# First element by seven products, its first pair's weights on their own, and three moves in the slots' order

## The chip, the cores and the metric

The kernel runs on one core of one Trainium2 chip. The metric is device time in microseconds (us) of one execution. Before the change the median of three runs is 3424.11 us (3422.17 to 3424.67). The profile comes from one further execution.

## The reference, cut to what matters

Everything is float32: 32 elements of 512 nodes with 512 features, each with its own 512 x 512 adjacency. Layer 0 is an attention with 8 heads of 64, whose weights are multiplied by the adjacency; layer 1 is a graph attention.

```python
q = x @ Wq.T + bq;  k = x @ Wk.T + bk;  v = x @ Wv.T + bv          # heads of 64
attn = softmax(q @ k.T / 8 + log(clip(adj, 1e-8)))                 # per head
x = layer_norm(x + (attn @ v) @ Wo.T + bo)
p = x @ fc_w.T + fc_b
l = (p @ q_w + q_b) + (p @ k_w + k_b).T + (1 - adj) * -1e9
out = softmax(leaky(l)) @ p + x
```

## The kernel before, in words

**Slots.** For each element b the four pairs of heads p go through slot(b, p), so there are 4 x 32 slots, the very last of which is last_slot. In one slot TensorE does the scores of pair p (score, L821, four tiles "sc"), the attention times v of the pair before it (values, L859, "po"), and the projections q and k of the next pair. Layer 1 of the element before is woven between. The order on each engine is the order in which the code calls the helpers: the schedule is manual and every engine takes its instructions in that order. Almost every helper puts work on several engines, so moving one call moves its part on TensorE (PE), VectorE (DVE), ScalarE (ACT) and the queue of SP, through which all DMAs go.

**Exponentials and factors.** ScalarE takes exp of each score tile into a tile "at" (L826). VectorE multiplies it by the clipped adjacency, held transposed in the tile cT (factors, L834); cT is loaded in blocks (load_a, L514) and turned in place (turn_a, L566). VectorE also adds the at tiles over keys ("as", L844 and L847).

**Products by four and by seven.** A product of two 2 x 2 block matrices can be done by four 128x512-wide accumulations or, with sums and differences of blocks, by seven half as wide (instead of eight). For elements 1 to 31 seven_qk (L613, into the banks a, b, c, d of two "f" tiles) and seven_v (L206, "pv_a", "pv_b", "pv_c") do this. They need three differences of blocks of x, the tile T, which differences (L594 to L597) makes, together with a change of xT in place; and three combinations of the weights, qk_s and v_s, which combine_units (L181 to L184) makes, with a change of wk and wv in place. After the products VectorE adds banks into qT, kT (L645 to L647) and v (L682, L686, L687). combine_right (L196 to L199) makes the same combinations for fc, "fc_s".

Element 0 is done otherwise: qk_units and v_units (L311, "pq", "pk", "pv") with plain products of x and whole weights. The weights' combinations stand in slot 0 of element 0 (the last one, on wk, in slot 3).

**Loads.** SP issues x of element 0 (four pieces), two biases, wq in four pieces, wk, wv (1 MB each), then the 16 block loads of the adjacency, and then wo, fc and the small rows (load_first_constants, load_a, load_constants).

**Layer 1 around the change.** layer1_rows is the rest of slot 2: it normalises the element before (L367 on ScalarE), forms its dots with uk and uq (L377, with a junk output), stores k's row to DRAM (store_k), loads it back to all partitions (load_k, into a tile "w"), and transposes the next x (L544). For b = 1 it also ends with combine_right of fc. In slot 3, softmax gives three units: logits of rows 0 and 1, of rows 2 and 3 (ScalarE L420 then VectorE L421), and weights (L427 to L432).

**The last slot.** It has layer 1 of elements 30 and 31. soft[1] of element 30 stands behind values and a first product of out. The dots of element 31 write their junk into the tile w, which is in the one buffer of tag "x" that the transposed weights eT of element 30 hold before it, read by its products z ("pz", L311). "pt_e" are transposes of the softmax weights (L304), "pg" the last products (L311), "pw" the products with wo.

Two lines show where the first element differs:

```python
next_qk = qk(0, p + 1)                   # b == 0 and p < 3
next_qk = seven_qk(b, p + 1)             # else, p < 3
```

## Time and profile before

| what | value |
|---|---|
| median of three runs | 3424.11 us (3422.17 to 3424.67) |
| profiled execution, its own time | 3423.87 us |
| its span, first to last instruction | 3422.1 us |
| TensorE busy | 3399.8 us, 99% |
| VectorE busy | 2991.7 us, 87% |
| ScalarE busy | 1392.2 us, 41% |
| DMA | 73 GB/s mean |
| mean granted TensorE clock | 0.998 |

A line of the timeline has the start in us, the duration in us, the engine, the line of the kernel, the operation, out<-in by the program's names, shapes and count, and in brackets the idle time before it with what ended it. A line of the waits has the engine and line that waited, what it waited for, the us in total, the number of times and the longest. A row of the windows has a stretch of time, then each engine's busy us and its instructions, the granted clock (1.00 is full speed), the DMA share and GB/s. A TensorE product in float32 shows two records for each call, so a product of four calls is "x8".

### The profile page before, as it was taken

The numbers are of one execution on the slowest core, as the hardware profiler recorded it, in microseconds if no ns is written. First come the engines' busy times: TensorE is split into PE (matmuls) and PEld (weight loads), VectorE is DVE, ScalarE is ACT, GpSimd is POOL, SyncE is SP. The second block draws the span as 40 slices with busy tenths as digits, with TensorE's granted clock in tenths as the row PEclk, the third lists the DMA queues.
The fourth block names the chain that finished last, engine by engine and source line by source line (L and its number), as shares of the span: only waits on it lengthen the run. The fifth ranks groups of instructions, "written<-read, shape, count | busy, mean of one in ns | idle before, by whom it ended". The sixth has DMA issues, their size and how long they took to land.

```text
span 3422.1 us, 42719 instructions
## 1 busy us (share of the span) xinstructions
PE 3399.8 (99%) x15250; PEld 2331.8 (68%) x15250; DVE 2991.7 (87%) x5239; ACT 1392.2 (41%) x2368; POOL 0.9 (0%) x9
## 2 busy tenths in 40 slices
PE   9999999999999999999999999999999999999998
PEld 3667776776677667766776677677767776776654
DVE  5889989889898898888898988989889989889885
ACT  3444443434433444434444343443344443434432
POOL 0000000000000000000000000000000000000000
PEclk9999999999999999999999999999999999999999
DMA  4244233342423433333424234343344343342420
GB/s 117 38 78 90 60 81 69 63 90 64 86 66 57 90 81 68 79 64 69 90 60 87 67 58 90 71 79 72 53 87 87 62 82 67 63 90 63 86 75 32
DMA packets 880034, 250.93 MB, mean 73 GB/s; under 512 B 806732, under 2 KB 806988, under 8 KB 879816
## 3 DMA queue, kind: packets, MB, share of 16 engines
q1 hardware_dynamic: 879816, 248.15, 35.8%
q8 instruction: 122, 2.00, 0.2%
q14 instruction: 96, 0.79, 0.1%
HBM read 181.93 MB, written 34.65 MB: 63 GB/s over the span
## 4 chain that ended last, share of the span: by engine, by line
PE 97%; DVE 1%; ACT 0%; DMA 0%; issue 0%; SPq 0%; DVEq 0%
PE f L613 22%; PE sc L821 14%; PE po L859 13%; PE pw_a L206 7%; PE pw_z_a L986 6%; PE pv_a L206 5%; PE pw_o_a L206 4%; PE pw_c L206 3%; PE pv_c L206 3%; PE pv_b L206 3%; PE pw_z_c L986 3%; PE pw_o_c L206 3%; PE pw_o_b L206 3%; PE ps L876 2%; PE pw_b L206 2%; PE pw_z_b L986 2%
## 5 line engine op out<-in xcount | busy, mean ns | idle before, releaser
L826 ACT ACTIVATE at<-sc 128x1024 f32<-128x1024 f32 x512 | 496.6, 1022 | 597.5 <-PE sc L821 596.2
L834 DVE SCALAR_TENSOR_TENSOR at<-cT,at 128x1024 f32<-128x1024 f32 x512 | 600.2, 1214 | 18.0 <-ACT at L826 17.6
L821 PE MATMUL sc<-qT,kT 64*128 64x512 f32 x2048 | 508.8, 615 | 1.4 <-DVE kT L647 1.4
L859 PE MATMUL po<-at,v 128*64 128x512 f32 x2048 | 468.1, 599 | 0.4 <-DVE at L834 0.3
L821 PEld LDWEIGHTS sc<-qT,kT 64*128 64x128 f32 x2048 | 177.7, 186 | 269.1 <-issue 269.1
L859 PEld LDWEIGHTS po<-at,v 128*64 128x64 f32 x2048 | 135.4, 136 | 317.4 <-issue 311.8
L847 DVE TENSOR_TENSOR as<-as,at 128x1024 f32<-128x1024 f32 x254 | 310.2, 1221 | 5.4
L613 PE MATMUL f<-xT,wq 128*128 128x256 f32 x992 | 261.7, 386 | 0.0
L613 PE MATMUL f<-T,qk_s 128*128 128x256 f32 x992 | 244.5, 379 | 0.0
L613 PEld LDWEIGHTS f<-xT,wq 128*128 128x128 f32 x992 | 183.9, 190 | 74.7 <-ACT at L826 52.0
L986 PE MATMUL pw_z_a<-eP,n 128*128 128x256 f32 x960 | 226.9, 379 | 1.1 <-DVE n L1023 1.1
L613 PEld LDWEIGHTS f<-T,qk_s 128*128 128x128 f32 x992 | 188.3, 190 | 25.9
L986 PEld LDWEIGHTS pw_z_a<-eP,n 128*128 128x128 f32 x960 | 180.2, 190 | 28.3 <-ACT L L998 1.5
L867 ACT COPY oT<-po 128x512 f32<-128x512 f32 x128 | 75.2, 587 | 290.0 <-PE po L859 290.0
L844 DVE TENSOR_TENSOR as<-at,at 128x1024 f32<-128x1024 f32 x128 | 154.9, 1210 | 1.1
L636 ACT ACTIVATE qT<-f,bq 128x256 f32<-128x256 f32 x124 | 58.3, 470 | 220.1 <-PE f L613 220.1
L642 ACT ACTIVATE kT<-f,bk 128x256 f32<-128x256 f32 x124 | 58.5, 472 | 195.8 <-PE f L613 195.8
L752 DVE TENSOR_TENSOR n<-pw_a,n 128x512 f32<-128x512 f32 x96 | 66.4, 691 | 77.0 <-PE pw_a L206 77.0
L613 PE MATMUL f<-T,wk 128*128 128x256 f32 x496 | 127.3, 379 | 0.0
L613 PE MATMUL f<-xT,qk_s 128*128 128x256 f32 x496 | 127.3, 379 | 0.0
L613 PE MATMUL f<-xT,wk 128*128 128x256 f32 x496 | 127.3, 379 | 0.0
L206 PE MATMUL pv_a<-wv,xT 128*128 128x256 f32 x496 | 120.4, 386 | 0.0
(255 smaller groups left out, 5804.5 us busy)
## 6 DMA issues: line engine op xcount, KB each, us to landing
cT<-in_adj_dram SPq DMA_DIRECT2D x512, 64.0 KB
R<-d SPq DMA_DIRECT2D x126, 256.0 KB
x<-in_x_dram SPq DMA_DIRECT2D x124, 256.0 KB
n<-in_x_dram SPq DMA_DIRECT2D x31, 1024.0 KB
L<-in_adj_dram SPq DMA_DIRECT2D x60, 512.0 KB
eP<-L SPq DMA_DIRECT2D x480, 64.0 KB
out_dram<-yb SPq DMA_DIRECT2D x58, 512.0 KB
w<-dk SPq DMA_DIRECT2D x32, 256.0 KB
```

Source lines behind the costliest of these rows:

```text
L206: nc.tensor.matmul(to[:, n, :], data(i, c)[:, ts(n, P)], weights[i][:, c, :], start=(first and n == 0 and c == 0), stop=(n == KH - 1 and c ...
L613: nc.tensor.matmul(to, left[i][:, c, ts(p, P)], s["B"][i][:, c, :], start=(first and c == 0), stop=(c == KH - 1), skip_group_check=True,)
L752: nc.vector.tensor_add(to, ps[name], to)
L821: nc.tensor.matmul(sc[:, j, :], s["kT", p][rows, ts(kc, P)], s["qT", p][rows, :], start=True, stop=True,)
L826: nc.scalar.activation(at, sc, AF.Exp, scale=SCALE)
L834: nc.vector.scalar_tensor_tensor(at, cT[:, kc, :].unsqueeze(1).to_broadcast([P, 2, N]), ADJ_MIN, at, ALU.max, ALU.mult,)
L844: nc.vector.tensor_add(s["as", p], s["at", p, 0], s["at", p, 1])
L847: nc.vector.tensor_add(s["as", p], s["as", p], s["at", p, kc])
L859: nc.tensor.matmul(s["po", p][j * DK : (j + 1) * DK, :], s["v"][h // 4][:, kc, ts(h % 4, DK)], s["at", p, kc][:, j, :], start=(kc == 0), s ...
L867: nc.scalar.copy(s["oT"][p], s["po", p])
L876: nc.tensor.matmul(ps[h * BL : (h + 1) * BL, :], ones[:, :BL], s["as", p + h // 2][:, h % 2, :], start=True, stop=True,)
L986: nc.tensor.matmul(ps[name][:, m, :].rearrange("p (c n) -> p c n", c=KH), left[i][:, t, ts(m, P)], right[i][:, :, ts(t, P)], start=(first ...
```

## The change

It has five parts:

- **Loads.** The first 128 columns of wq and wk, all that pair 0 of element 0 needs, are loaded on their own into "first_pair", a tile from the ring of six "at" buffers. After them wv, wq and wk come whole, in this order, each as one DMA.
- **Element 0.** Pair 0's q and k are plain products with these columns. differences(0) and all combinations of wv, wq and wk follow at once, ahead of turn_a. v is then done by seven products (two units in slot 0 between the scores, two after them), and q and k of pairs 1 to 3 by seven_qk.
- **combine_right of fc** (slot 2 of element 1) stands ahead of the additions of next_qk, no longer at the end of layer1_rows.
- **soft[1] of element 30** in the last slot stands between the two halves of values.
- **The dots of element 31** write their junk into the tile R of that element; the tile w is taken only for load_k.

```diff
-    def load_first_constants():
+    def load_first_constants(pair):
         K["bq"] = load_col(const, bq, "bq")
         K["bk"] = load_col(const, bk, "bk")
-        K["wq"] = load_weight(wqT, "wq", 4)
+        for dst, w in zip(pair, (wqT, wkT)):
+            nc.sync.dma_start(out=dst, in_=w[:, :P].rearrange("(c p) d -> p c d", p=P))
+        K["wv"] = load_weight(wvT, "wv")
+        K["wq"] = load_weight(wqT, "wq")
         K["wk"] = load_weight(wkT, "wk")
-        K["wv"] = load_weight(wvT, "wv")
...
-            run(values(b, p - 1) if p > 0 else values(last, 3) if last >= 0 else first_v[1:2])
+            run(values(b, p - 1) if p > 0 else values(last, 3) if last >= 0 else first_v[:2])
...
-                if b == 0:
-                    run(combine_qk()[1:])
...
-            if b == 0 and p < 3:
-                next_qk = qk(0, p + 1)
-            elif p < 3:
+            if p < 3:
                 next_qk = seven_qk(b, p + 1)
...
                 if b == 0:
-                    run(combine(K["wv"], K["v_s"])[:1] + combine_qk()[:1])
-                run(next_qk)
-                if b == 0:
-                    run(first_v[2:] + combine(K["wv"], K["v_s"])[1:])
+                    run(first_v[2:] + next_qk)
                 else:
+                    run(next_qk)
...
             if b == 1:
+                combine_right(K["fc"], K["fc_s"])
                 run(next_qk[2:])
...
-            if b == 1:
-                combine_right(K["fc"], K["fc_s"])
...
             vs[0]()
+            soft[1]()
             vs[1]()
             rest[0]()
-            run(soft[1:])
+            run(soft[2:])
...
-            ks, qs = dots(b)
+            ks, qs = dots_units(S[b], small, S[b]["R", 0][:, 1, :], b)
             run(ks)
-            k_rows(b)
+            store_k(S[b], small, dram, b)
+            load_k(S[b], work(b)[:, 1, :])
...
-        load_first_constants()
+        pair = act.tile([P, 2, N], FP, tag="at", name="first_pair", bufs=6)
+        pair = [pair[:, i, :].rearrange("p (c d) -> p c d", c=DC) for i in range(2)]
+        load_first_constants(pair)
...
-        first_v = v(0)
-        run(qk(0, 0) + first_v[:1])
+        run(first_qk(*pair))
+        differences(0)
+        run(combine(K["wv"], K["v_s"]) + combine_qk())
+        first_v = seven_v(0)
         turn_a(range(NC))
```

More of the change, by code (lines that the diff above doesn't have):

```diff
@@ L320, in v_units, with qk_units @@
         return [lambda c=c: unit(c) for c in range(NC)]
-    def qk_units(s, wk, p, qT, kT, psum, name):
+    def qk_units(s, wq, wk, p, qT, kT, psum, name):
         def unit(w, b, to, what):
@@ L328, in qk_units @@
         return [
-            lambda: unit(K["wq"], K["bq"], qT, "q"),
+            lambda: unit(wq, K["bq"], qT, "q"),
             lambda: unit(wk, K["bk"], kT, "k"),
@@ L575, in qk_tiles, with first_qk @@
                 S[b][w, p] = act.tile([P, N], FP, tag=w, name=f"{w}_{b}_{p}", bufs=2)
-        def v(b):
-            v_tiles(b)
-            return v_units(S[b], K["wv"], ps_m, b)
-        def qk(b, p):
-            qk_tiles(b, p)
-            s = S[b]
-            return qk_units(s, K["wk"], p, s["qT", p], s["kT", p], ps_m, b)
+        def first_qk(wq, wk):
+            qk_tiles(0, 0)
+            s = S[0]
+            return qk_units(s, wq, wk, 0, s["qT", 0], s["kT", 0], ps_m, 0)
         def differences(b):
@@ L1082, in work @@
             return S[b]["w"]
-        def dots(b):
-            w = work(b)
-            return dots_units(S[b], small, w[:, 0, :], b)
-        def k_rows(b):
-            store_k(S[b], small, dram, b)
-            load_k(S[b], S[b]["w"][:, 1, :])
         def softmax(b):
@@ L1443, in general @@
             kT = act.tile([P, N], FP, tag="kT", name=f"g_kT_{p}")
-            for u in qk_units(s, s["wk"], p, qT, kT, ps_m, "g"):
+            for u in qk_units(s, K["wq"], s["wk"], p, qT, kT, ps_m, "g"):
                 u()
```

## The prediction

> **What bounds the kernel now.** I read the page's busy shares first, then the list of what TensorE waited for over the whole span, then the timeline of each wait with the engine that ended it, and last the granted clock around them.

> ```profile
> PE 3399.8 (99%) x15250; PEld 2331.8 (68%) x15250; DVE 2991.7 (87%) x5239; ACT 1392.2 (41%) x2368; POOL 0.9 (0%) x9
> ```
> ```profile
> PE pt_x L560 <- DMA n<-in_x_dram: 3.7, 1, 3.7
> PE pv_c L206 <- DVE T L594: 2.6, 1, 2.6
> PE pt_e L304 <- ACT cT L432: 2.5, 4, 1.4
> PE pk L311 <- DMA wk<-in_wkT_dram: 2.3, 1, 2.3
> PE sc L821 <- DVE kT L647: 1.4, 1, 1.4
> ...
> PE pw_c L206 <- DVE oT L928: 1.1, 1, 1.1
> ```

> TensorE is busy 99%, and each of these waits happens once (the third in four pieces): at the start, in slot 2 to 3 of element 1, and in the last slot. Between them the kernel is TensorE's work end to end, 52.5 us an element, and the diff changes no instruction of elements 2 to 30. So I price four places: the loads, element 0, element 1, the tail.

> ```profile
> 13.63 5.37 PE L311 MATMUL pk<-xT,wk 128*128 128x512 f32 x8 [2.34 <-DMA wk<-in_wkT_dram]
> 18.83 3.60 PE L311 MATMUL pv<-wv,xT 128*128 128x512 f32 x8
> ```
> ```profile
> 174.30:176.80 2.50, 0.00 (x1) 0.00 (x0) 2.47 (x4) 1.55 (x3) 0.00 (x0) 1.00 0.90 344
> 176.80:178.00 1.20, 1.13 (x4) 0.99 (x5) 1.13 (x3) 0.27 (x1) 0.00 (x0) 0.85 0.06 21
> 178.00:179.00 1.00, 1.00 (x4) 0.79 (x3) 1.00 (x3) 0.00 (x0) 0.00 (x0) 0.50 0.00 0
> ```
> In the second fence, the third figure from the right is the granted clock (0.50 in the last row). **An idle TensorE costs twice**: after the waits of 2.34 and 2.57 us it runs at half clock for about 4 us. pk takes 5.20 us to the next start, 18.83 - 13.63, where the same eight records later take 3.44: 1.76 lost. pv_c and the two f products after it take 4.38 (176.87 to 181.25) against 2.58: 1.80 lost. After the 1.35 us wait before sc at 164.89 the clock stays 1.00, so the step lies between 1.4 and 2.3 us of idleness.

> [...]

> **The change, part by part.**

> *Loads.* All go through SP's one queue. The two pair tiles (256 KB each, runs of 512 B) stand where the first two 256 KB pieces of wq stood. pq never waited for those: its second quarter started at 8.44. Price of the pair's 0.52 MB: runs of 2 KB move 314 to 385 GB/s in the first 15 us, the 128 B runs of cT some 115; so 1.5 us to 4.6. Per run that is 94 and 17.8 ns on each of 16 engines; a straight line between gives 33 ns for 512 B, 248 GB/s, 2.1 us, which I take. pq then starts 0.2 late (0 to 1.3), and pk finds its weights. All of wv, wq, wk and adjacency land 2.1 later: the transposes of cT (L566), now at 18.19, 20.09, 22.14 and 24.50, can go up to 26.6.

> [...]

> *Element 0, slot 0.* Before: pk's issue ends at 18.83. After: 7.58 + 0.2 + 2 x 3.44 = 14.66, **-4.17** (wait, lost clock, and 0.27 of drain that the wait was counted from). From there to the scores of pair 1 it was 43.76 - 18.83 = 24.93. Now: kT is no longer covered by pv, so sc waits for ScalarE, 0.2 + 0.69 + 0.15 = 1.04; four score tiles 3.82; seven v products at 1.725 (pv_b to pv_a, 93.29 to 95.02) 12.08 in place of four at 3.44; seven f products at 0.865, 6.05 in place of two at 3.44; changes of tile 0.2; and the additions into kT before sc, 1.1 (in slot 2 of element 1 the same handover takes 1.52 from the last f record's slot to sc, with ScalarE busy on other rows). Sum 24.29, **-0.64**.

> VectorE must keep up. It does three differences under pq, the fourth after pk (14.9), combine of wv 4 x 0.72 to 18.4, of wq and wk 4 x 1.24 from about 18.7 to 23.7 (wk lands about 18.6), the transposes to 27.3, four factors at 1.17, one sum 1.22, three v additions 1.95: 35.2. TensorE's last f product ends at 37.6. Slack 2.0 us: up to 2.0 more of load delay is free.

> *Slots 1 to 3.* Slot 1: f 6.05 for 6.87, -0.82; f now waits for the second exponential to free its bank, +0.45; the additions end under ps_bvwo (3.44), so sc does not wait. **-0.37.** Slot 2: **-0.82**, the additions under ps_bfc. VectorE runs about 1.0 us later against TensorE in slot 2, so T's first difference comes 0.15 late for pv_c in slot 3: **+0.15**; the one operation on wk leaves that slot (-1.22 on VectorE), and its 3.38 us of idleness before L682 absorbs the rest. If it did not, up to 1 us more.

> Element 0 together: -4.17 - 0.64 - 0.37 - 0.82 + 0.15 = **-5.85** (bounds -3 and -7).

> *Element 1, slot 2.*

> ```profile
> 163.66 0.42 DVE L645 TENSOR_TENSOR qT<-f,qT 128x256 f32<-128x256 f32 x1 [3.62 <-ACT kT L642]
> ...
> 173.48 0.69 DVE L196 TENSOR_TENSOR fc_s<-fc 128x512 f32<-128x512 f32 x1
> ...
> 175.53 0.68 DVE L199 TENSOR_TENSOR fc<-fc 128x512 f32<-128x512 f32 x1
> 176.14 0.68 DVE L594 TENSOR_TENSOR T<-xT 128x512 f32<-128x512 f32 x1
> ```
> The four operations of combine_right stand ahead of the difference that pv_c waits for. Moved before the additions of next_qk they take 2.7 us inside the 3.62 that VectorE stands idle for ScalarE's kT; behind them wait only L645 to L647. If they overran, sc would wait up to 2.7 longer. T starts at 173.48 and pv_c at 174.25 instead of 176.87: 2.62, and the clock's 1.80: **-4.4** (bounds -2.6 without the clock, -4.5). Late next: the copy into pv_b behind the w activations on ScalarE, at 177.1, needed at 177.7.

> *Tail.*

> ```profile
> 3331.96 0.69 DVE L421 CUSTOM_DVE_ANT_0 qk_s<-w,qk_s 128x512 f32<-128x512 f32 x1 [2.42 <-ACT w L420]
> ...
> 3336.00 0.75 DVE L476 SCALAR_TENSOR_TENSOR yb<-pg,r,yb 128x512 f32<-128x512 f32 x1
> ...
> 3368.07 0.69 DVE L377 SCALAR_TENSOR_TENSOR w<-n,uk 128x512 f32<-128x512 f32 x1 [2.92 <-PE pz L311]
> ```
> soft[1] ahead of vs[1]: its ScalarE activations no longer queue behind oT, which waits for po until 3330.72; they run at 3328.1, right after the exponentials, and L421 goes at 3329.5. The weights end at 3333.6; then L476 waits for pg until 3334.3 instead of starting at 3336.00. VectorE runs unbroken from there to pw_c: **-1.7**, with TensorE now waiting 1.5 at pw_c instead of 1.12. oT is not delayed: the activations end at 3329.4.

> Dots into R: L377 waited for pz because tile w takes the buffer that pz reads. Into R the first dot follows the mask, at 3365.2: **-2.87**. load_k still needs that buffer, but pz ends 3.4 us before SP issues it; SP's order of store_k, load_k and the stores of out stays, as the moved operations issue no DMA. All up to the exponentials of cT (L432) and pt_e is this one chain: dots, sums, residual, L476, L421, weights. TensorE's pg end moves only by 1.7 plus the 0.66 it waits for yb, to 3379.9, still ahead of the last exponential at 3381.6. Fewer gaps ahead of pt_e: before, 1.40 and three of 0.38 sum to 2.54, and the clock from 3386.5 to 3389 is 0.50; now some 1.2, like the 1.07 of pt_e at 3335 to 3337, after which thirteen records take 2.21 instead of 2.83. With pz, **-0.8** (0 to -0.9). Tail -5.4 (bounds -2.9 and -5.5).

> **Sum.** -5.85 - 4.4 - 5.4 = -15.6. The profiled execution took 3423.87 us (span 3422.1 and 1.8 around it), 0.24 under the median of the runs: 3423.87 - 15.6 = **3408.3**.

> **Rivals.**
> 1. *Element 0 becomes VectorE's.* If the pair costs 4.6, pq starts 1.3 late, cT comes 2.5 later than I take and 0.5 passes the slack; with waits of 1 us at three pair ends in place of those priced, the start gives -3: 3411.2. For it: twelve VectorE operations now stand before the first factor. Against: 15 us of idleness in its first 25. Chance 0.18.
> 2. *The tail is held elsewhere.* The 1.5 us gap at pw_c halves the clock (1.8), or the copy of dk through DRAM returns no earlier, and only 2.9 comes: 3410.8. Against it: w lands 3.2 us after its issue with nothing else in the queue. Chance 0.14.
> 3. *Adjacency far too late, slower.* Place: the end of slot 0. wq and wk now go whole ahead of cT, and every factor waits for all four transposes. Each us beyond the 2.0 of slack costs one, plus 1.8 of clock; from about 16 us of delay the gain is gone, at 24 the time is 3423.87 - 15.6 + 22 + 1.8 = 3432. The rows speak against it: 4.19 MB landed in 15 us. Chance 0.02.
> 4. *The change doesn't do what it says*: the pair is waited for as long as wk was and the tail's moves free nothing, so only the product counts (1.66 + 3 x 0.82 = 4.1, less 2.7 of new gaps) and element 1's 4.4 remain: 3418.1. Against it: bytes ahead of pk are halved. Chance 0.03.

> **How the numbers follow.** The forecast itself, 3406 to 3410, 0.63. The range reaches to rivals 1 and 2 and a us of the runs' spread below: 3405.5 to 3413. A measurement of this kernel tells 0.2% (6.8 us) from no change; faster is the forecast and rivals 1 and 2, 0.95; within it, rival 4, 0.03; slower, rival 3, 0.02.

> **What would show it.** Right: no wait of pk for DMA, pk at clock 1.00; scores of pair 1 near 38.9 us; fc_s ahead of L645 and no wait of pv_c for T; L377 without a wait for pz; pt_e at clock 1.00. Wrong: TensorE waiting for VectorE at the ends of slots 0 to 2, a half clock at pw_c, or an element period other than 52.5 us.

## The result and the profile after

The changed kernel takes 3411.05 us (median of seven runs, 3409.84 to 3411.89); the kernel before took 3422.67 (seven runs on the same chip, 3422.17 to 3424.67). The ratio is 0.9964, interval 0.9953 to 0.9976: 11.6 us faster. The profiled execution took 3410.55 us, its span is 3408.7, so between the two profiles lie 13.3 us of the 15.6 forecast.

The page's busy shares and, below, the list of what TensorE waited for over the whole span:

```profile
PE 3391.4 (99%) x15310; PEld 2340.6 (69%) x15310; DVE 2998.9 (88%) x5255; ACT 1393.5 (41%) x2374; POOL 0.9 (0%) x9
```
```profile
PE pt_x L563 <- DMA n<-in_x_dram: 4.1, 2, 3.6
PE sc L820 <- DVE kT L646: 2.3, 2, 1.4
PE pw_c L209 <- DVE oT L927: 1.2, 1, 1.2
...
PE sc L820 <- ACT kT L330: 0.8, 1, 0.8
PE f L612 <- ACT f L629: 0.8, 1, 0.8
PE pt_e L307 <- ACT cT L435: 0.8, 2, 0.4
```

Three of the old waits are gone or cut: pk for wk (2.3), pv_c for T (2.6), and pt_e for cT from 2.5 to 0.8. New are sc for the first kT (0.8), a second sc for kT (0.9 of the 2.3) and f for a copy by ScalarE (0.8). TensorE is busy 8.4 us less.

Stage by stage, each length read as the distance between the same two products on both timelines (pk's end is the next product's start before, 18.83, and after, where a wait follows it, its first record plus 3.44):

| stage | forecast | measured |
|---|---|---|
| start to the end of pk's issue | -4.17 | -2.70 (18.83 to 16.13) |
| slot 0 of element 0 behind it | -0.64 | -0.63 |
| slots 1, 2, 3 | -0.37, -0.82, +0.15 | -0.43, -0.82, 0.00 |
| element 1 | -4.4 | -3.09 (88.83 to 85.74) |
| element 2 to the scores of the last slot | 0 | +0.08 |
| last slot | -5.4 | -5.8 |
| sum | -15.6 | -13.4 |

So two stages gave less: the start by 1.47 and element 1 by 1.31. The timeline of the start:

```profile
6.05 1.97 PE L563 MATMUL pt_x<-ident,n 128*128 128x128 f32 x8 [0.49 <-DMA n<-in_x_dram]
8.06 4.80 PE L314 MATMUL pq<-xT,first_pair 128*128 128x512 f32 x8
12.69 3.60 PE L314 MATMUL pk<-xT,first_pair 128*128 128x512 f32 x8
17.07 1.99 PE L820 MATMUL sc<-qT,kT 64*128 64x512 f32 x8 [0.78 <-ACT kT L330]
```

pk has no wait, as forecast. But x came in two parts, so pq starts 0.48 later than before, and pq takes 4.63 to pk's start where pk takes 3.44 for the same eight records. The rows of the windows show that these records are slow although the granted clock, the third figure from the right, is printed as 1.00 (four records in the first 2 us, six in the later):

```profile
8.00:10.00 2.00, 1.97 (x4) 0.91 (x4) 1.90 (x4) 0.49 (x2) 0.00 (x0) 1.00 0.90 298
...
12.00:14.00 2.00, 2.00 (x6) 0.80 (x6) 0.00 (x0) 0.69 (x1) 0.00 (x0) 1.00 1.05 409
```

That 1.00 is no measurement. The trace keeps the granted clock as entries, each with its start, its length and its share of full speed. The column counts time without an entry as full speed, and in this execution the first entry, of full clock, starts at 10.30 us. The spacing of pq's records changes at that moment: 1.01, 0.85 and 0.62 us up to the record at 10.54, 0.43 from there. The same holds in all fourteen profiles of this document (e1 to e12 are described below):

| profiles | first entry of full clock, us | pq to pk, us |
|---|---|---|
| before, e2, e3, e4, e10 | 6.86 to 7.91 | 3.51 to 3.54 (before: its eight records, then the wait) |
| e1, e6 | 9.01, 9.01 | 4.09, 4.36 |
| changed kernel | 10.30 | 4.63 |
| e5, e7, e8, e9 | 11.56 to 12.11 | 5.15 to 5.63 |
| e11, e12 (TensorE warmed up) | 5.85, 5.34 | 3.51, 3.52 |

So pq runs at half speed until full clock is granted: its records stand 0.85 us apart ahead of the entry and 0.43 behind it, as pk's in the kernel before stand 0.85 apart under a granted clock of 0.50 (14.46 to 17.02). The kernel before was profiled in an execution in which full clock came early, at 6.97.

The timeline of element 1, slots 2 and 3, from the combination of fc to the next kT:

```profile
155.37 0.68 DVE L199 TENSOR_TENSOR fc_s<-fc 128x512 f32<-128x512 f32 x1
...
168.90 0.69 DVE L593 TENSOR_TENSOR T<-xT 128x512 f32<-128x512 f32 x1
169.64 1.99 PE L209 MATMUL pv_c<-v_s,T 128*128 128x256 f32 x8
...
177.18 0.36 ACT L629 COPY f<-f 128x256 f32<-128x256 f32 x1
177.59 1.13 PE L612 MATMUL f<-T,qk_s 128*128 128x256 f32 x4 [0.78 <-ACT f L629]
```

fc_s stands in the gap and pv_c no longer waits: it starts 7.23 earlier than before, of which 4.58 came from element 0, so 2.65 is won here (2.62 forecast). But from pv_c to the scores of element 2 it is 17.85 against 18.29 before: only 0.44 of the lost clock's 1.80 comes back. The last line shows a new wait of f.

Three lines of the last slot: the residual yb at once when pg allows it, the first dot without a wait for pz, and pt_e's thirteen records in 1.66 us (3.04 before).

```profile
3326.75 0.75 DVE L479 SCALAR_TENSOR_TENSOR yb<-pg,r,yb 128x512 f32<-128x512 f32 x1 [0.77 <-PE pg L314]
...
3355.82 0.68 DVE L380 SCALAR_TENSOR_TENSOR R<-n,uk 128x512 f32<-128x512 f32 x1
...
3373.89 1.66 PE L307 MATMUL pt_e<-ident,cT 128*128 128x128 f32 x13 [0.38 <-ACT cT L435]
```

### The profile page after: what moved, and what is told of

Read it like the earlier page. It is cut to its first block, busy times and chain, and to the rows that moved or that the text cites. A ratio compares the mean times of both kernels' runs of the same rounds, so it can differ in the third digit from the quotient of the medians.

```text
span 3408.7 us, 42865 instructions
## 1 busy us (share of the span) xinstructions
PE 3391.4 (99%) x15310; PEld 2340.6 (69%) x15310; DVE 2998.9 (88%) x5255; ACT 1393.5 (41%) x2374; POOL 0.9 (0%) x9
## 4 chain that ended last, share of the span: by engine, by line
PE 97%; DVE 2%; SPq 0%; ACT 0%; issue 0%; DMA 0%; DVEq 0%
PE f L612 22%; PE sc L820 14%; PE po L858 13%; PE pw_a L209 7%; PE pw_z_a L985 6%; PE pv_a L209 5%; PE pw_o_a L209 4%; PE pw_c L209 3%; PE pv_b L209 3%; PE pv_c L209 3%; PE pw_z_c L985 3%; PE pw_o_c L209 3%; PE pw_o_b L209 3%; PE ps L875 2%; PE pw_b L209 2%; PE pw_z_b L985 2%
```

## The experiments

Each of e1 to e9 and e11 is one execution, read by the distance between two products; its time stands beside 3422.4 to 3422.8 for the kernel before on the same chip. "sc(b,p)" are the first scores of pair p of element b.

**e1: the combination of fc back at the end of layer1_rows.**

```diff
             if b == 1:
-                combine_right(K["fc"], K["fc_s"])
                 run(next_qk[2:])
...
             run(adds[3][:1] + qs + adds[3][1:])
+            if b == 1:
+                combine_right(K["fc"], K["fc_s"])
```

> The changed kernel with combine_right of fc back at the end of layer1_rows of element 1. In the changed kernel TensorE's scores of element 2, pair 0, start 85.74 us after those of element 1, pair 0 (101.75 to 187.49); before it was 88.83. Theory (the move gained 3.09, because only a part of the 4.4 from wait and clock was kept): 88.8 here, pv_c waits 2.6 for T and runs at half clock, the span grows by 3.1. Rival (the whole 4.4 came from the move and something else in the change cost 1.3 in this element): 90.1. This kernel also shows the start a second time: if pq's first records run at half speed by chance of the run, pk's first record starts 3.4 to 4.6 us after pq's; if the 512 B runs of the pair cause it, 4.6 again and pq again near 8.06.

3412.34 us. sc(1,0) to sc(2,0) is 88.83 (101.01 to 189.84), to the hundredth the length before: element 1's whole 3.09 is this one move. Its pv_c on the timeline, and two windows, the second of them the stretch over which the clock was halved:

```profile
171.56 2.56 PE L209 MATMUL pv_c<-v_s,T 128*128 128x256 f32 x8 [2.57 <-DVE T L593]
```
```profile
169.43:172.85 3.42, 1.29 (x6) 1.17 (x7) 3.32 (x6) 1.82 (x3) 0.00 (x0) 1.00 0.51 195
172.85:176.26 3.41, 3.41 (x10) 2.70 (x9) 3.41 (x5) 0.59 (x1) 0.00 (x0) 0.50 0.14 24
```

**e2: soft[1] of element 30 back behind the first product of out.**

```diff
             vs[0]()
-            soft[1]()
             vs[1]()
             rest[0]()
-            run(soft[2:])
+            run(soft[1:])
```

> The changed kernel with soft[1] of element 30 back behind values and the first product of out. Marker: from the last first-product pg of out (element 29, the eight records in the last slot) to pw_c of element 31; 14.81 us in the changed kernel (3323.01 to 3337.82), 16.46 before. Theory (VectorE's unbroken chain from the weights to oT sets pw_c): 16.5, and everything behind shifts by 1.65. Rival (the move only let VectorE wait for pg sooner, and dots in R alone set the rest): 14.8 to 15.0. The start is shown a third time.

3411.65 us. From pg to pw_c 16.45 (3322.28 to 3338.73) against 14.81 in the changed kernel: the move is worth 1.64.

**e3: the dots of element 31 back into tile w.**

```diff
-            ks, qs = dots_units(S[b], small, S[b]["R", 0][:, 1, :], b)
+            w = work(b)
+            ks, qs = dots_units(S[b], small, w[:, 0, :], b)
...
-            load_k(S[b], work(b)[:, 1, :])
+            load_k(S[b], w[:, 1, :])
```

> The changed kernel with the dots of element 31 writing their junk into w again. Marker: from pw_c of element 31 to the first pz record behind pt_e; 37.56 us in the changed kernel (3337.82 to 3375.38), 41.90 before. Theory (dots wait for pz 2.9 us, and the gaps ahead of pt_e grow so that the clock halves and costs 1.3 more): 41.9, granted clock near 0.5 over the thirteen pt_e records. Rival (the clock's step there is chance): 40.5, clock 1.00. The start is shown a fourth time.

3414.12 us. From pw_c to pz 41.60 (3336.80 to 3378.40) against 37.56: 4.04. The first dot waits for pz again:

```profile
3357.80 0.69 DVE L380 SCALAR_TENSOR_TENSOR w<-n,uk 128x512 f32<-128x512 f32 x1 [2.92 <-PE pz L314]
```

The thirteen records of pt_e take 2.72, behind a wait of 1.40 for the exponential, and the granted clock falls to 0.50 at 3376.27, after the first four of them. So the length lies between the theory's 41.9 and the rival's 40.5, nearer to the theory: the clock does fall, but not for all thirteen.

**e4: the kernel before with the new loads alone** (plain products throughout).

```diff
+        for dst, w in zip(pair, (wqT, wkT)):
+            nc.sync.dma_start(out=dst, in_=w[:, :P].rearrange("(c p) d -> p c d", p=P))
+        K["wv"] = load_weight(wvT, "wv")
-        K["wq"] = load_weight(wqT, "wq", 4)
+        K["wq"] = load_weight(wqT, "wq")
         K["wk"] = load_weight(wkT, "wk")
-        K["wv"] = load_weight(wvT, "wv")
...
-        run(qk(0, 0) + first_v[:1])
+        run(first_qk(*pair) + first_v[:1])
```

> The kernel before with the first pair's columns loaded on their own and the order wv, wq, wk; element 0 stays with plain products by four, and no move in later slots. Theory (the load takes away the wait of 2.34 and the half clock of pk, less what pq loses at its start): the scores of pair 0 start at about 19.6 (pk's end 16.1 and one pv of 3.44) if pq is as slow as in the changed kernel, 18.4 if pq runs at full speed; before 22.36. The later distances stay as before: 83.97 from there to the scores of element 1. Rival (pq's late start and slow records come from the 0.48 us later x, which the pair's queue place causes): pq starts near 8.06 and takes 4.6 here too.

3420.59 us. pq started at 7.65, pk at 11.19 without a wait and at full speed, sc(0,0) at 18.15, sc(1,0) at 102.12: 4.21 earlier than before, the forecast's -4.17. By chance it showed more, in element 1, which it does not change. Its wait for T, and two windows cut like those of e1:

```profile
172.65 1.99 PE L208 MATMUL pv_c<-v_s,T 128*128 128x256 f32 x8 [2.57 <-DVE T L601]
```
```profile
170.70:174.12 3.42, 1.47 (x7) 1.32 (x8) 3.35 (x6) 1.82 (x3) 0.00 (x0) 1.00 0.54 207
174.12:177.53 3.41, 3.41 (x18) 3.00 (x17) 3.41 (x4) 0.59 (x1) 0.00 (x0) 1.00 0.13 20
```

The wait is as long as in e1, and the clock stays at 1.00. Yet sc(1,0) to sc(2,0) is 88.38, only 0.45 less than with the half clock, and f then waits 0.78 for its copy. So the half clock behind this wait was mostly covered by what VectorE and ScalarE do there.

**e5: the changed kernel with the loads of before.**

```diff
-        for dst, w in zip(pair, (wqT, wkT)):
-            nc.sync.dma_start(out=dst, in_=w[:, :P].rearrange("(c p) d -> p c d", p=P))
-        K["wv"] = load_weight(wvT, "wv")
-        K["wq"] = load_weight(wqT, "wq")
+        K["wq"] = load_weight(wqT, "wq", 4)
         K["wk"] = load_weight(wkT, "wk")
+        K["wv"] = load_weight(wvT, "wv")
...
-        run(first_qk(*pair))
+        run(first_qk(K["wq"], K["wk"]))
```

> The changed kernel with the loads of before (wq in four pieces, wk, wv) and no pair tile; pair 0 takes its columns from the whole wq and wk. The seven products of element 0 and the three moves stay. It tells whether the load alone made the start's gain or the products need it. Theory (the load is worth the wait of pk and its half clock; the products and new gaps are worth -1.9 by themselves): pk waits 2.3 for wk, the scores of pair 0 start near 19.8 (pk's slot to 18.8 and 0.94), those of element 1 at 84.68 after that, as in the changed kernel, so near 104.5. Rival (products by seven need the late wv, and VectorE's combinations then hold TensorE): v_s comes later than pv_a ends and pv_c waits more than 0.5 us, element 1 starts at 105.5 or later.

3411.34 us. The wait of pk for wk that I expected did not come:

```profile
8.33 5.31 PE L312 MATMUL pq<-xT,wq 128*128 128x512 f32 x8 [0.40 <-DMA wq<-in_wqT_dram]
13.48 3.60 PE L312 MATMUL pk<-xT,wk 128*128 128x512 f32 x8
```

pq ran slowly here too, without the pair's loads, until 13.48, by when wk had landed. The slow pq is thus not the pair's doing; full clock came at 11.63 here. Where pq is this slow the pair's loads win nothing: in e7, e8 and e9, with the pair and full clock as late, pk starts at 13.28 to 13.49. What the loads are worth on average over executions no run tells. The other theory, that v_s comes late, fell as well: VectorE waits 0.38 for wv, TensorE not at all.

**e6, e7, e8: element 1's new wait.** e6 puts the logits (soft[1]) behind next_qk[0], so that ScalarE's copy goes first; e7 puts the sums over keys behind the additions of next_qk; e8 does both, all for b = 1 alone (the conditions on b are left out here).

```diff
-                run(soft[1:2])
                 next_qk[0]()
+                run(soft[1:2])             # e6, e8
...
-                sums(b, 2, 1)
                 vs[2]()
                 run(next_qk[2:])
+                sums(b, 2, 1)              # e7, e8
```

> The changed kernel with soft[1] of element 0 (in slot 3 of element 1) behind next_qk[0], so that ScalarE copies bank a of f into b before the logits that wait for VectorE. It tells what took back a part of element 1's gain. From the scores of element 1, pair 0, to those of element 2: 85.74 in the changed kernel. Theory (VectorE's queue from T to the additions into kT is unbroken and sets the scores): the wait of 0.78 for the copy goes, but the scores wait for kT instead, 85.6 to 85.8. Rival (ScalarE's order alone held TensorE): 84.5 to 84.8.

> The changed kernel with the sums of pair 2 of element 1 (two VectorE additions, 2.4 us) behind the additions of next_qk in slot 3 of element 1. Distance as in the run before, 85.74 in the changed kernel. Theory (both queues hold TensorE, ScalarE's copy first): VectorE's additions into kT come 2.4 earlier, the wait of 0.78 for the copy stays, only the last 0.2 goes, 85.5. Rival (VectorE alone): 84.5 to 84.8.

> The changed kernel with both: soft[1] behind next_qk[0] and the sums behind its additions, in slot 3 of element 1. Theory (the 1.2 us that the prediction counted and the run did not give sit in these two queues in series): no wait of f for the copy, scores right behind pv_a, 84.5, which is 1.24 less than the changed kernel and 4.3 less than before. Rival (a third thing holds it, the logits' transfer or T): 85.2 or more.

e6, 3409.68 us: f's wait is gone, and sc(1,0) to sc(2,0) is 85.73, where it was 85.74: sc(2,0) waits instead.

```profile
186.47 1.99 PE L820 MATMUL sc<-qT,kT 64*128 64x512 f32 x8 [1.17 <-DVE kT L646]
```

e7, 3411.91 us, and e8, 3411.98: from sc(1,0) to sc(1,3) these two took 58.89 and 58.92, where the changed kernel took 58.56, ahead of the edits and for a reason I have not found; so I count from sc(1,3), from where the changed kernel takes 27.18 to sc(2,0). e7 takes 26.98 and keeps f's wait, e8 26.30. Each alone gives 0 or 0.20, both 0.88: two chains end within a quarter of a us of each other. Over the whole distance e8 took 85.22, where its theory had 84.5 and its rival 85.2 or more; counted from sc(1,3), 0.88 of the theory's 1.24 came. The rest is probably here, on e8's timeline; no run moved it:

```profile
186.05 0.46 ACT L641 ACTIVATE kT<-f,bk 128x256 f32<-128x256 f32 x1
...
187.77 1.99 PE L820 MATMUL sc<-qT,kT 64*128 64x512 f32 x8 [0.31 <-DVE kT L646]
```

ScalarE's part of kT stands behind four exponentials (L435) and a v activation (182.73 to 186.1), and VectorE's additions wait 1.43 for it.

**e9: the pair's columns in runs of 128 bytes**, four times as many.

```diff
-            nc.sync.dma_start(out=dst, in_=w[:, :P].rearrange("(c p) d -> p c d", p=P))
+            for i in range(4):
+                nc.sync.dma_start(out=dst[:, :, ts(i, 32)],
+                                  in_=w[:, ts(i, 32)].rearrange("(c p) d -> p c d", p=P))
```

> The changed kernel, with the first pair's columns loaded in runs of 128 bytes (four transfers of 32 columns each per matrix) in place of 512. The same bytes in four times the runs: worked out from the rows of the kernel before, the pair takes about 2.5 us longer in the queue. Theory (VectorE has slack behind the scores of the first pair, 4.4 us idle ahead of its f additions in the changed kernel): pq waits for the pair and pk starts 1 to 2 us later; wk and cT land about 2.5 us later (VectorE's wait for wk ends near 21.4 instead of 18.9, the last cT transposition is near 28.7 instead of 26.2), and nothing behind it moves: sc(0,0) to sc(0,1,0) stays 23.36 and sc(0,0) to sc(1,0) stays 84.68. Rival (the prediction's first rival, the pair's loading pushes wk and cT past what covers them): sc(0,1,0) waits more than its 1.10 and the distance from sc(0,0) is over 23.8.

3411.51 us. The two DMA waits on VectorE's timeline:

```profile
20.06 1.23 DVE L186 TENSOR_TENSOR qk_s<-wk 128x1024 f32<-128x1024 f32 x1 [1.32 <-DMA wk<-in_wkT_dram]
...
27.03 0.71 DVE L571 STREAM_TRANSPOSE cT<-cT 128x512 f32<-128x512 f32 x1 [0.29 <-DMA cT<-in_adj_dram]
```

wk comes 1.2 later than in the changed kernel (18.85) and the last of cT 0.85 later (26.18): half and a third of what I expected. pq did not wait for the pair at all, and pk's late start (13.47) is again pq's slow records (5.46 to pk). From sc(0,0) to the scores of pair 1 it is 23.37 and to sc(1,0) 84.68, as in the changed kernel: the slack behind slot 0 covers the delay that there was. The 2.5 us that the forecast's first rival takes were not reached even so.

**e10 and e12: the stages put together.** e10 is the changed kernel with e8's edit (not repeated here) and with one product of v ahead of the first scores and one behind q and k of pair 1:

```diff
-            ... else first_v[:2])
+            ... else first_v[1:2])
...
-                    run(first_v[2:] + next_qk)
+                    run(first_v[2:3] + next_qk + first_v[3:])
...
         first_v = seven_v(0)
+        run(first_v[:1])
         turn_a(range(NC))
```

> The changed kernel with both moves of the element 1 experiments, and in the first slot one product of v put ahead of the first scores and one behind q and k of the second pair, where PE waits 0.94 and 1.10 now. Theory (these two waits are only a lack of work in the right place): pk's first record to sc(1,0) falls from 89.06 to about 87.0, sc(1,0) to sc(2,0) from 85.74 to about 84.9, in sum 2.9 less; the median 3408.1 (3406.9 to 3409.3), 0.9992 of the changed kernel. Rival (as in element 1, the wait comes back at the next thing that VectorE or ScalarE does in order): pk to sc(1,0) stays above 88.5 and the median within 1 us of the changed kernel's 3411.05.

3409.05 us (five runs, 3407.43 to 3411.18), 0.9961 of the kernel before, interval 0.9947 to 0.9974. Neither of the first two waits for kT is left; on TensorE's timeline both score groups follow without a bracket:

```profile
18.60 1.99 PE L820 MATMUL sc<-qT,kT 64*128 64x512 f32 x8
...
37.51 1.99 PE L820 MATMUL sc<-qT,kT 64*128 64x512 f32 x8
```

pk's start to sc(1,0) is 87.21 (89.06 in the changed kernel), sc(1,0) to sc(2,0) 84.85 (85.74): 2.74 of the 2.9 expected.

**e11 and e12: TensorE warmed up.** e11 is the changed kernel, e12 is e10, each with eight transpositions that nobody reads:

```diff
+        warm = ps_s.tile([P, 2, N], FP, tag="s", name="warm")
+        for i in range(8):
+            nc.tensor.transpose(warm[:, 0, :P], ident, ident)
         first_xT()
```

The two test whether work of TensorE ahead of x brings the first entry of full clock forward, and with it pq's full speed; "cold clock" stands for the slow records ahead of that entry.

> The changed kernel with eight transpositions of the identity by TensorE, into a PSUM tile that nobody reads, between the making of the identity (1.4 us) and the landing of x (3.6 us). In the runs so far the transpositions of x took 0.245 us each and pq's first records had twice their spacing in all runs in which x landed in two pieces. [...] Rival (the loads' traffic, or the weights' own reading, holds pq up): pq to pk stays 4 to 5.6 with records at twice the spacing, and sc(0,0) is at 16.5 to 17.9.

> The kernel with all four moves, with the eight transpositions ahead of x as well. Theory of the cold clock: pk starts at about 11.2 to 11.8 instead of 12.3 on average, and the median is 0.5 to 1.5 us below that of the kernel with the four moves alone (about 3407). Rival (the start's slow records have another cause): the two medians are within 0.4 us of each other.

The start of e11:

```profile
1.46 1.97 PE L1384 MATMUL warm<-ident 128*128 128x128 f32 x8 [1.46 <-POOL eps L107]
3.46 1.97 PE L563 MATMUL pt_x<-ident,n 128*128 128x128 f32 x8
5.86 1.44 PE L563 MATMUL pt_x<-ident,n 128*128 128x128 f32 x8 [0.43 <-DMA n<-in_x_dram]
7.67 3.67 PE L314 MATMUL pq<-xT,first_pair 128*128 128x512 f32 x8 [0.38 <-ACT xT L565]
```

3408.76 us. Full clock was granted from 5.85, in e12 from 5.34, earlier than in any of the twelve profiles without warming. The second half of pt_x takes 1.44, in e12 1.36; in the eight runs without warming in which it stood apart it took 1.93 to 1.97. (x landed in two parts in e2 too, and pq took 3.51 there, so the slow records do not come with two parts in every run.) pq reaches pk in 3.51, and the scores of pair 1 start at 38.92, where the forecast had 38.9. e12: 3407.69 us (five runs, 3406.96 to 3409.63), 0.9956 of the kernel before, interval 0.9943 to 0.9970. It is the lowest median of all, 1.36 under e10 on the same chip, but the times of the two overlap, and so do the intervals of e12 and the changed kernel. It is the lengths of the stages, not the times, that show the gain, and for the start they are two profiles.

## Why the prediction was nearly right

The direction, the places and most of the mechanisms held; the forecast was 2.75 us low against the median. The time alone could not have told: 3411.05 lies beside the 3411.2 and 3410.8 of rivals 1 and 2, and neither of them happened. By its own steps:

- **Loads: right in price, wrong in what they free.** wk reached VectorE at 18.85 (18.7 forecast) and the last of cT at 26.18, 1.68 later than before (2.1 forecast, up to 26.6). The step that failed is "After: 7.58 + 0.2 + 2 x 3.44 = 14.66". It took pq at the full speed that the one trace of before showed, and it was chance that full clock came early there (6.97): pq took 3.51 to 3.54 in five of the twelve profiles without warming and 4.1 to 5.6 in the seven in which it came later. pk of the runs with the pair and no edit at the start began between 11.20 and 13.49. A slow pq in the kernel before would have been hidden behind the wait for wk (to 13.63), as e5 hides it; the changed one shows it. e11 brings the step back: pk's end is 11.18 + 3.44 = 14.62.
- **Element 0: right.** Slots 0 to 3 are within 0.15 each, and sc(0,0) to sc(1,0) is 84.68 to 84.69 in every run of the changed kernel's order. VectorE's slack behind slot 0 was 4.4 us, not 2.0 (it stands idle for that long ahead of L644 at 39.17): v's additions were done at 34.78. The working's own figures, 35.2 and 37.6, give 2.4.
- **Element 1: the wait right (-2.65), the clock wrong.** The failing step is "2.62, and the clock's 1.80". A stretch of slow TensorE is worth its loss only if nothing else limits the same stretch. Here f's bank waits for a ScalarE copy and sc for VectorE's additions; of the 1.80, 0.44 was on the path. e4 showed it from the other side, at 0.45. The forecast looked at what is "late next" and named another copy behind the same activations, as just in time; f's copy stands in that same queue.
- **Tail: right, 0.4 too small.** soft[1] gave -1.65 (-1.7 forecast). The dots gave, with pt_e, -4.34 against -2.87 and -0.8. The mis-sized term is "thirteen records take 2.21": in the rows that it was read from, a wait of 0.42 stands inside these records. Here, at clock 1.00 throughout and without such a wait, they took 1.49 from the first one's start to pz, against 2.83 before. What follows pt_e took 0.2 longer than before. The half clock at pw_c of the second rival did not come (a gap of 1.24).
- **Rivals.** The first fell: the pair did not cost 4.6, and e9's further delay of about 1 us moved nothing behind sc(0,0). The second fell with the tail's two numbers, the third and fourth with the time itself.

The clock itself: behind equal waits of 2.57 us it was 0.50 in e1 and in the kernel before, and 1.00 in e4. The forecast drew from its rows that "the step lies between 1.4 and 2.3 us of idleness", and e4's wait is longer than that. The traces' entries of the clock show what the waits differ in. Within one profile all changes lie whole multiples of 3.413 us apart; in the kernel before they are at 6.97, 13.79, 17.21, 177.63, 181.05, 3386.16 and 3389.58, which is 2, 1, 47, 1, 939 and 1 times that. Each half clock ahead of the end of the program lasted 3.41 (the forecast's "about 4 us"). Below, a stretch is the 3.413 us from one such multiple to the next, counted on between the changes. In the kernel before the first border behind the start of the span would lie at 0.14, in e1 at 2.18.

The stretches right ahead of the six falls had 2.05 to 2.57 us of idleness: in the kernel before 2.34 (pk), 2.57 (pv_c) and 2.40 (pt_e), in e1 2.12, in e3 2.05, in e4 2.19 (pt_e). The border between two stretches cut e4's wait for T into 0.62 and 1.95, and the clock stayed at 1.00; no other stretch that ended between the first full clock and the last product had more than 1.4. (The first windows shown with e1 and e4 are such stretches: TensorE is busy 1.29 and 1.47 us there.) So in these profiles, between those two, the clock fell behind every stretch with 2.05 us of idleness or more and behind none with 1.95 or less. The three waits of 2.57 us differ in the border: it left the one in the kernel before whole (174.30 to 176.87, in the stretch from 174.22 to 177.63) and cut 0.44 off e1's.

Open: what decides whether x lands in one part or in two; what sets the place of the stretches against the start of an execution; what brings the first full clock (in e10 it came behind a stretch with 2.83 us of work, in e8 not behind one with 3.07); and the 0.1 to 0.36 us between sc(1,0) and sc(1,3) in e3, e7, e8 and e9.

## What to carry to other kernels

A wait that is taken away at the start exposes what it covered: ask what the profile cannot show because the wait hides it, and whether one profile is typical of it. Check the clock column against the spacing of equal records, above all at the start. A stretch of slow clock is priced like any other length, by what limits the stretch, not by its own loss (in element 1 0.44 of 1.80). Where one removal gives nothing, look for a second chain that ends at the same time and move both, as e6, e7 and e8 did.
